# A graph attention layer on one core: weights loaded beside the projections, and the first sort, turn and chain put elsewhere

## The chip, the cores and the metric

The kernel runs on one core of a Trainium2 chip. The metric is the device time of one execution in microseconds (us), as the median of several runs; less is better. A core has TensorE (PE; its weight loads are listed as PEld), VectorE (DVE), ScalarE (ACT), GpSimd (POOL) and SyncE (SP). They run their own instruction queues in order and wait for each other by semaphores. SP, ACT and POOL also issue DMA transfers; "ACTq" is an instruction of ACT's queue that is not computation.

## The reference

One layer of a graph network on 4096 nodes of 512 features, with 8 heads of 64. The adjacency matrix is 4096 x 4096 of int32 with about 0.4% ones (made symmetric, with the diagonal), so a row has some 8 to 39 neighbours.

```
hs = layer_norm(x) * ln1_scale + ln1_bias ;  ht = layer_norm(h_target) * ln1_scale + ln1_bias
q = (ht @ Wq + bq) / 8 ;  k = hs @ Wk + bk ;  v = hs @ Wv + bv
probs = softmax over s of (q . k, where adj[t, s] != 0)          # per head
ht = layer_norm(ht + (probs @ v) @ Wo + bo) * ln2_scale + ln2_bias
out = _layernorm(x + ht + gelu(ht @ W1) @ W2)                    # W1: 512 x 2048, W2: 2048 x 512
```

All of it is in float32.

## The kernel before

The kernel doesn't multiply full matrices of 4096 x 4096: it makes neighbour lists out of the adjacency, sorts the target rows by their number of neighbours, and gathers the k|v rows of the neighbours slot by slot. P is 128; a row tile is 128 rows, so there are 32.

**Stage 1, projections** (`project`, L853). x is read two row tiles at a time. `measure` takes means and variances on DVE, `scale` normalizes on ACT, `turn` transposes on PE and copies out of PSUM with scale and bias on ACT (L896), `source` multiplies with Wk and Wv on PE (L906; an fp32 matmul is recorded as two), copies the result to an SBUF tile `tq` on ACT (L908) and writes 128 rows of k|v to the DRAM table `kvd` by a DMA of ACT's queue (L910). The gathers of attention need the whole table.

**Stage 1, lists** (`edges`, L703). A tile's adjacency comes in four quarters of 128 x 1024 by DMAs of SP's queue (L700) into slots of a ring of 17 buffers `kv` of 128 x 1024 floats; DEEP of them are used for that. ACT takes the sign and counts (L715), DVE multiplies with an index and takes maxima (L720, L722) and merges candidates (L729 to L746). The target rows are read beside it for their moments (`moments`, into ring slots by `hrow`). After the lists of the first 16 tiles (part A), `prepare` takes the moments of all targets and calls `sort(0)` (L794): one-hot rows of the degree (L814), counts by matmuls with ones and a running sum on DVE (L825, L826), ranks within a degree by matmuls with a lower triangle (L833, L834), and the rank (L837, L839). POOL then scatters the records of part A to DRAM, one DMA for each of 16 tiles (L842). `first_fronts` reads the first records, gathers target rows, normalizes them on ACT (L967), turns them and makes q (L980, L982). Meanwhile `fill` does lists of FILL = 5 tiles of part B.

**Stage 2, attention** (`attention`, L1104). The sorted tiles form 17 groups: one tile with 11 slots, then pairs with a nearly constant sum. A step has up to S = 3 slots. `issue` (L1001) gathers, by an indirect DMA of POOL's queue for each slot (L941), 128 rows of k|v into the ring, AHEAD = 4 steps before use. DVE multiplies with q (L1158) and reduces to logits `lg` (L1162), ACT takes exponentials (L1166, L1176) and weighs one slot of v (L1141), DVE the others (L1121), and PE adds up over transposes in PSUM (L1129). `finish` (L1021) is a generator: the chain at the end of a tile (sums, context, Wo, second norm, turned rows `h2T`), cut in pieces by `yield`, of which `advance` runs one each time, twice a step, so that no engine waits in its queue for the chain.

**Stage 2, feed forward** (`feed`, L1251). When a group's `h2T` is there, PE does `hidden` (L1266), ACT gelu (L1269), PE `output` (L1275), and `end` closes the rows with a norm and a scatter to the output. W1 and W2 are kept in four quarters, of 1 MB each from either matrix. `load_quarter` loads quarters 0 and 1 on SP's queue beside projections 8 and 10; `weights`, a stream of stage 2, loads 2 and 3 on ACT's queue. The memory of quarter 3's pool (`s2wb`, right side) and of quarter 2's (`s2wa`) is free only when the pools of stage 1 are closed: `wp` with R0 (the records of part A), `ip`, and `kvw` with Wk and Wv.

**Order.** `_weave` runs the streams of a stage by virtual time: a `yield` of a cost puts its stream later. That gives the order in which instructions are written; a planner of the framework then orders each engine's queue by that order, by what is ready, and by its own estimates of durations. In the last weave `other_lists` does the remaining tiles and `sort(1)`.

## Time and profile before

| | |
|---|---|
| median of 6 runs | 1877.92 us (1874.34 to 1881.0) |
| the profiled execution | 1879.3 us, span 1877.5 us |
| granted PE clock, mean | 0.967 |
| busy: PE, DVE, ACT, POOL | 1696.5 (90%), 1432.3 (76%), 1247.2 (66%), 890.5 (47%) us |
| moved by DMA | 463.28 MB, mean 247 GB/s |

Times in the profile are us from the span's start. A row of the timeline has start, duration, engine, line, operation, output and inputs with their shapes, how many were merged, and in brackets how long the engine was idle before and who released it. The releaser is inferred from semaphores: where several are waited for, the last one is named. A row in the table of stretches gives each engine's busy time and number of instructions, the clock that TensorE was granted (1.00 is full), the mean busy share of the 16 DMA engines, and GB/s. A busy PE isn't always PE at its peak, as matmuls are pipelined.

Landmarks: the projections' first matmul starts at 15.73, the lists of part A end at 197.5, rank is there at 245.3, the last k|v rows are issued at 300.5, the first gather at 308.7; attention starts on DVE at 319.5, the first feed at 375.0, the second at 448.4, and the last output row is scattered at 1863.

### The profile page before, as it was taken

What the parts mean: (1) busy time and instruction counts of PE and PEld (TensorE: products, weight loads), DVE (VectorE), ACT (ScalarE), POOL (GpSimd) and SP (SyncE); (2) the same over time, 40 slices, a digit from 0 to 9 for tenths busy, and PEclk for the clock granted to TensorE, in tenths of its full rate; (3) what the DMA queues carried; (4) which work ended last, traced back from release to release, by engine and by line L of the source; (5) the groups of instructions that cost most, each with busy time, mean ns of one, the idle gap of its engine ahead of it and who ended that gap; (6) DMA issues with size and microseconds to landing.
All of it is one profiled execution on the core that took longest, in us unless ns stands there. A gap on an engine that the chain in (4) does not pass through costs nothing. (4 is left out here: it accounts for less than half of the span.)

```text
span 1877.5 us, 22938 instructions
## 1 busy us (share of the span) xinstructions
PE 1696.5 (90%) x7030; PEld 1092.6 (58%) x7030; DVE 1432.3 (76%) x2591; ACT 1247.2 (66%) x3139; POOL 890.5 (47%) x804
## 2 busy tenths in 40 slices
PE   7989884598998989999989989899999999999996
PEld 3444331465666657666666656566666666656664
DVE  7989854989998838787878889888877878777400
ACT  6767634577886737777777777677767677777411
POOL 1000143746445474656566666655555555655101
PEclk9999987799999989999999999999999999999998
DMA  9999958878877657778778788777677867666000
GB/s 347 359 387 372 354 164 312 322 263 316 319 272 254 208 161 235 257 245 269 254 262 270 261 269 290 242 245 247 214 240 230 266 201 249 225 219 223 23 1 24
DMA packets 147757, 463.28 MB, mean 247 GB/s; under 512 B 24468, under 2 KB 29160, under 8 KB 147624
## 3 DMA queue, kind: packets, MB, share of 16 engines
q0 software_dynamic: 95696, 342.19, 53.8%
q1 hardware_dynamic: 44112, 96.44, 14.6%
q10 hardware_dynamic: 7816, 23.08, 3.2%
q8 instruction: 58, 0.95, 0.2%
q14 instruction: 75, 0.61, 0.1%
HBM read 430.76 MB, written 30.89 MB: 246 GB/s over the span
## 5 line engine op out<-in xcount | busy, mean ns | idle before, releaser
L941 POOL DMA_INDIRECT kv<-kvd,rec x603 | 690.2, 1145 | 487.3 <-PE cps L1129 205.4
L1266 PE MATMUL pf<-h2T,w 128*128 128x256 f32 (+1 forms) x2176 | 472.1, 369 | 2.2 <-issue 1.6
L1275 PE MATMUL po<-w,gt 128*128 128x512 f32 x1024 | 469.4, 599 | 0.3 <-issue 0.3
L1158 DVE TENSOR_TENSOR kv<-kv,tq 128x1536 f32<-128x1536 f32 (+2 forms) x211 | 352.4, 1676 | 112.5 <-DMA kv<-kvd,rec 82.5
L1266 PEld LDWEIGHTS pf<-h2T,w 128*128 128x128 f32 x2176 | 388.6, 191 | 66.3 <-issue 22.0
L1141 ACT ACTIVATE kv<-kv,pa 128x64 f32<-128x64 f32 x1520 | 391.5, 336 | 3.7
L1162 DVE TENSOR_REDUCE lg<-kv 128x24 f32<-128x1536 f32 (+2 forms) x211 | 350.7, 1669 | 1.8 <-ACT pa L1138 0.3
L1129 PE MATMUL cps<-ident,kv 128*128 128x128 f32 x2008 | 263.9, 278 | 59.5 <-DMA kv<-kvd,rec 20.5
L1129 PEld LDWEIGHTS cps<-ident,kv 128*128 128x128 f32 x2008 | 236.4, 143 | 135.7 <-issue 83.8
L1275 PEld LDWEIGHTS po<-w,gt 128*128 128x128 f32 x1024 | 188.1, 193 | 189.5 <-issue 188.8
L1121 DVE TENSOR_TENSOR kv<-kv,p 128x1024 f32<-128x1024 f32 (+1 forms) x211 | 249.6, 1190 | 46.3 <-ACT p L1166 33.7
L674 POOL TENSOR_TENSOR n_rs<-n_ve,mhalf 128x2 f32<-128x2 f32 (+2 forms) x51 | 51.6, 1011 | 331.9 <-DVE n_ve L667 132.4
L1269 ACT ACT_TABLE_LOAD x111 | 142.4, 1283 | 1.7
L980 PE MATMUL t<-wq,tq 128*128 128x512 f32 x256 | 121.1, 617 | 16.7 <-ACT tq L974 12.8
L906 PE MATMUL pq<-wk,h2T 128*128 128x512 f32 x256 | 124.0, 628 | 11.6 <-ACT h2T L896 6.2
L722 DVE MAX8 cand<-sg 128x8 uint16<-128x103 uint16 (+1 forms) x640 | 130.8, 252 | 0.7
L1269 ACT ACTIVATE gt<-pf 128x512 f32<-128x512 f32 x128 | 76.4, 597 | 72.4 <-PE pf L1266 58.5
L906 PE MATMUL pq<-wv,h2T 128*128 128x512 f32 x256 | 118.3, 604 | 6.8 <-ACT tq L908 6.8
L1056 PE MATMUL t<-wo,rb 128*128 128x512 f32 x256 | 118.3, 606 | 1.4 <-DVE rb L1046 1.4
L715 ACT ACTIVATE sg<-kv 128x1024 uint8<-128x1024 int32 x84 | 88.6, 1056 | 43.5 <-DVE cand L722 20.6
L906 PEld LDWEIGHTS pq<-wk,h2T 128*128 128x128 f32 x256 | 50.2, 203 | 77.3 <-issue 58.6
L1166 ACT ACTIVATE p<-lg 128x24 f32<-128x24 f32 (+2 forms) x179 | 33.7, 188 | 91.5 <-DVE lg L1162 73.3
(154 smaller groups left out, 1601.2 us busy)
## 6 DMA issues: line engine op xcount, KB each, us to landing
kv<-in_adj_dram SPq DMA_DIRECT2D x84, 512.0 KB
a<-in_adj_dram SPq DMA_DIRECT2D x44, 512.0 KB
kvd<-tq ACTq DMA_DIRECT2D x32, 512.0 KB
kv<-kvd,rec POOLq DMA_INDIRECT x603
kv<-in_L_gnn_h_target_dram SPq DMA_DIRECT2D x32, 256.0 KB
kv<-in_x_dram SPq DMA_DIRECT2D x15, 512.0 KB
rest_d<-gid SPq DMA_DIRECT2D x32, 160.0 KB
w<-in_L_gnn_W_dram SPq DMA_DIRECT2D x4, 1024.0 KB
```

Source lines behind the costliest of these rows:

```text
L722: nc.vector.max(cand[:, h * SQ + s, :], wd[:, w0:w1])
L906: nc.tensor.matmul(pkv, hT[:, kc, j * P:(j + 1) * P], w[:, kc, :], start=kc == 0, stop=kc == KC - 1)
L941: nc.gpsimd.indirect_dma_start(out=dst, out_offset=None, in_=table[:, :], in_offset=bass.IndirectOffsetOnAxis(ap=idx, axis=0))
L980: nc.tensor.matmul(pq, hT[:, kc, :], wq[:, kc, :], start=kc == 0, stop=kc == KC - 1)
L1121: nc.vector.tensor_tensor(v4, v4, p[:, j0:j0 + m, :].unsqueeze(3) .to_broadcast([P, m, H, HD]), ALU.mult)
L1129: nc.tensor.matmul(cps[:, c, :], kv[:, j, D + c * P:D + (c + 1) * P], ident, is_transpose=True, start=j0 + j == 0 and c == 0, stop=j0 + n ...
L1141: nc.scalar.mul(v, v, pa[:, hd:hd + 1])
L1158: nc.vector.tensor_tensor(kv[:, :n, :D], kv[:, :n, :D], tq[:, :D].unsqueeze(1).to_broadcast([P, n, D]), ALU.mult)
L1162: nc.vector.tensor_reduce(lg[:, :n, :], kv[:, :n, :D].rearrange("p j (h d) -> p j h d", h=H), AX.X, ALU.add)
L1266: nc.tensor.matmul(pf[:, k, :], w1[(f0 + k) // KC][:, kc, (f0 + k) % KC * P:((f0 + k) % KC + 1) * P], h2T[:, kc, :w], start=kc == 0, stop= ...
L1269: nc.scalar.activation(gt, pf, AF.Gelu_apprx_tanh)
L1275: nc.tensor.matmul(po[j], gt[:, k, j * P:(j + 1) * P], w2[(f0 + k) // KC][:, (f0 + k) % KC, :], start=False, stop=f0 + k == FC - 1, skip_g ...
```

## The change

- Quarters 0, 1 and 2 of W1 and W2 are loaded on SP's queue beside projections 6, 8 and 10, in the pool `wp2`. The stream `weights` is gone. Quarter 3 is loaded on ACT's queue in `attention` at step 1, after two one-column copies on ACT that read that step's `lg`.
- To make room, the pools `wp` and `ip` are gone. Their tiles are now parts of ring slots 7 (constants and moments) and 11 (the records R0 and the one-hot rows of the first sort), or of the pool `sp`.
- The adjacency has 7 ring slots (0 to 6) instead of 8, the target rows 3 (8 to 10) instead of 4.
- When the target rows are done, `source` uses ring slots 8 to 10 for k|v instead of the three buffers `tq`.
- The first rows are copied out of PSUM by DVE instead of ACT in `turn(0)`.
- `advance` runs three pieces of a chain until the first `h2T` is there.
- `fill` starts 9 units of virtual time later.

```diff
-            DEEP = 8
+            DEEP = 7
...
+            first_rec = ring[:, 11, :NA * RW].bitcast(I32).rearrange("p (n w) -> p n w", w=RW)
+            first_oh = ring[:, 11, 512:512 + NB * NA // 2].bitcast(BF16)
...
-            def load_quarter(pool, q, engine=nc.sync):
+            def load_quarter(pool, q, engine=nc.sync, gate=None):
                 w1.append(pool.tile([P, KC, D], F32, name=f"w1_{q}"))
                 w2.append(pool.tile([P, KC, D], F32, name=f"w2_{q}"))
+                if gate is not None:
+                    nc.scalar.copy(w1[q][:, 0, 0:1], gate)
+                    nc.scalar.copy(w2[q][:, 0, 0:1], gate)
                 engine.dma_start(w1[q], W1[:, q * D:(q + 1) * D].rearrange("(c p) n -> p c n", p=P))
...
             def hrow(i):
-                return ring[:, DEEP + i // 2 % 4, i % 2 * D:(i % 2 + 1) * D]
+                return ring[:, 8 + i // 2 % 3, i % 2 * D:(i % 2 + 1) * D]
...
-                            nc.scalar.activation(hT[:, kc, :], pt[:, k, :], AF.Identity,
-                                                 bias=b1c[:, kc:kc + 1], scale=s1c[:, kc:kc + 1])
+                            if n == 0:
+                                nc.vector.tensor_scalar(hT[:, kc, :], pt[:, k, :],
+                                                        s1c[:, kc:kc + 1], b1c[:, kc:kc + 1],
+                                                        op0=ALU.mult, op1=ALU.add)
+                            else:
+                                nc.scalar.activation(hT[:, kc, :], pt[:, k, :], AF.Identity,
+                                                     bias=b1c[:, kc:kc + 1],
+                                                     scale=s1c[:, kc:kc + 1])
...
-                    kvr = sp.tile([P, 2 * D], F32, name="tq", bufs=3)
+                    if asked or moms:
+                        kvr = sp.tile([P, 2 * D], F32, name="tq", bufs=3)
+                    else:
+                        kvr = ring[:, 8 + (n * G + j) % 3, :]
...
                     for t in list(tails):
-                        if next(t, StopIteration) is StopIteration:
-                            tails.remove(t)
+                        for _ in range(1 if h2Ts or begun else 3):
+                            if next(t, StopIteration) is StopIteration:
+                                tails.remove(t)
+                                break
+                    if h2Ts:
+                        begun.add(True)
...
+                            if k == 1:
+                                load_quarter(s2wa, NQ - 1, nc.scalar, lg[:, 0, 0:1])
...
-                    if n in (8, 10):
-                        load_quarter(wp2, n // 2 - 4)
+                    if n in (6, 8, 10):
+                        load_quarter(wp2, n // 2 - 3)
...
                 while not ready:
                     yield None
+                yield 9.0
                 for cost in _take(ed, FILL * steps):
...
-            def weights():
-                for q, pool in enumerate(pools):
-                    yield 10.0
-                    load_quarter(pool, q + 2, nc.scalar)
...
-            _weave((att, 0), (chain(feed(g) for g in range(len(GROUPS))), 0), (other_lists(), WAIT),
-                   (weights(), 0))
+            _weave((att, 0), (chain(feed(g) for g in range(len(GROUPS))), 0), (other_lists(), WAIT))
```

## The prediction

> **What bounds the kernel now.** The chain that ended last was read first. Its 11 pieces all lie behind 1860 us of a span of 1877.5 and say nothing about the start, where every edit of this change lies. So the busy time by stretches comes next (columns: us; busy us and count of PE, PEld, DVE, ACT, POOL; granted PE clock; DMA share; GB/s).
>
> ```profile
> 140.00:180.00 40.00, 40.00 (x112) 19.02 (x111) 38.59 (x169) 30.56 (x57) 2.06 (x3) 1.00 1.00 370
> 240.00:260.00 20.00, 20.00 (x60) 9.66 (x59) 18.77 (x74) 9.57 (x18) 11.18 (x11) 0.99 0.31 104
> 260.00:280.00 20.00, 14.28 (x28) 5.85 (x27) 3.76 (x16) 6.16 (x12) 9.81 (x12) 0.83 0.60 177
> 280.00:300.00 20.00, 12.96 (x31) 5.78 (x30) 8.32 (x35) 10.34 (x22) 0.39 (x1) 0.87 0.69 230
> 300.00:320.00 20.00, 9.47 (x16) 3.46 (x14) 7.60 (x26) 6.23 (x12) 8.54 (x10) 0.76 0.99 345
> 320.00:340.00 20.00, 5.64 (x24) 4.84 (x24) 19.23 (x25) 7.21 (x31) 16.43 (x12) 0.52 1.03 410
> 480.00:600.00 120.00, 117.00 (x528) 80.24 (x527) 115.42 (x255) 99.18 (x241) 64.59 (x56) 1.00 0.84 292
> ```
>
> Until about 200 us PE and DMA are both full; from 480 on PE is full again. Between lies a hole: from 260 to 340 PE is busy 42 of 80 us and its clock falls to 0.52. What fills the hole is in the timeline, engine by engine.
>
> ```profile
> 172.42 0.60 PE L892 MATMUL t<-ident,kv 128*128 128x128 f32 x4
> 187.03 0.60 PE L892 MATMUL t<-ident,kv 128*128 128x128 f32 x4
> 235.48 0.48 PE L825 MATMUL t<-oh,ones_bf 128*128 128x384 bf16 x1 [6.56 <-DVE a L826]
> 269.17 6.31 PE L906 MATMUL pq<-wv,h2T 128*128 128x512 f32 x8 [5.72 <-ACT tq L908]
> 285.13 1.12 PE L971 MATMUL t<-ident,tq 128*128 128x128 f32 x4 [2.78 <-ACT tq L967]
> 374.97 0.80 PE L1266 MATMUL pf<-h2T,w 128*128 128x128 f32 x2
> 448.40 1.97 PE L1266 MATMUL pf<-h2T,w 128*128 128x256 f32 x4 [0.66 <-ACT h2T L1086]
> ```
>
> The first two rows give the pace of the projections when nothing holds them: one pair of row tiles in 14.6 us, back to back. So PE sets their end. The next three are its losses; the last two are the first group's feed forward (375) and the second's (448), from where PE stays full.
>
> ```profile
> 268.05 0.39 ACTq L573 DMA_DIRECT2D w<-in_L_gnn_W_dram  x1
> 268.54 0.59 ACT L908 COPY tq<-pq 128x512 f32<-128x512 f32 x1 [14.20 <-DMA rec<-R,ranki]
> 300.51 0.33 ACTq L910 DMA_DIRECT2D kvd<-tq  x1
> ```
> ```profile
> 245.78 1.74 POOL L842 DMA_INDIRECT rec<-R,ranki  x1 [39.21 <-DVE ranki L839]
> 308.71 0.94 POOL L941 DMA_INDIRECT kv<-kvd,rec  x1 [28.32 <-issue]
> ```
> ```profile
> 319.49 1.76 DVE L1158 TENSOR_TENSOR kv<-kv,tq 128x1536 f32<-128x1536 f32 x1 [3.95 <-DMA kv<-kvd,rec]
> ```
>
> ACT stood 14.20 us in front of a load of weights. It must be quarter 3: the memory of quarter 2 is that of Wk and Wv, in use until 295. That of quarter 3 holds R0, which the scatter of the records still reads. Behind it in ACT's queue lay the copy that empties PE's accumulators. The last k|v rows go out at 300.51; only then can POOL gather (308.71), and attention begins on DVE at 319.49.
>
> **The change, part by part.** Times are of this execution: 1879.3 us, span 1877.5, so 1.8 lie around it; it is 1.4 over the median 1877.92. Ends of each term stand in brackets; minus is a gain.
>
> First turned rows on DVE. The first projection starts at 15.73, behind ACT's scaling of the next rows at 14.41. The eight transposes end at 9.89. Four DVE operations of 128x256 from PSUM follow; the nearest rows are 0.56 for DVE's 128x384 from PSUM (L834) and 0.56 for ACT's own operation, so about 2 us: start near 11.6. PE then runs back to back, so all of it passes on: -4 [-5; 0 if the weights wk, issued at 2.87, land late]. DVE's wait for PE holds the next rows' statistics, which have 10 us of slack before their turn at 25.74.
>
> A third quarter beside the projections: 2.1 MB more where the DMA share is 1.00. SP's queue is moved past by two issues of 0.4 to 1.2 us; behind them are adjacency and x loads. The same load at 187 is followed by PE gaps of 0.70, 1.05 and 0.36 at 203 to 212; the one at 153 by none. At 370 GB/s it is 5.7 us of DMA. I take +2 [0; +5.7], as the rows of the like load are nearest. The ring of seven adjacency buffers instead of eight goes into that bound. The Trainium skill (DMA: Bandwidth & Descriptors, "Issuing engines are not separate DMA queues") says that transfers of all queues run on the same 16 DMA engines and interleave, so that nothing is won by the queue and a full stretch would pay the whole 5.7; by it the sum below would be -17.
>
> The first sort ahead of the lists. Now it takes from 198 to 245.3, with 214.59 to 234.50 between its one-hot rows and its scan, filled by list operations; PE waits 6.56 for that scan. From the turn at 219.16 to the one at 244.37 PE takes 25.2 instead of 14.6. Of these 10.6, some 1.7 are the sort's four matmuls, and waits in PE's order will leave some 3: -6 [-9; 0]. Rank and scatter should come 20 us earlier, which shortens nothing by itself: the gathers wait for the last k|v rows. The lists pushed back cost DVE time later (below).
>
> No weight load on ACT behind the scatter. From the turn at 258.98 PE needs three tiles of 6.87 and 0.87 for turning, so 280.5; the last matmul ends at 295.4: 14.9 lost. The 14.20 us hold gives 5.72 of waiting and 2.7 of half-rate matmuls (6.31 against 3.60). The rest is the first front: 2.78 of waiting, 1.0 of transposes, slow clock. With records 20 us earlier most of that goes too: -11 [-14; -4].
>
> Last k|v rows. From the last matmul to the first gather are 13.3 us, with a wait for a tq buffer (3.15) and a weight load in the same queue just ahead (297.26). The buffers in ring slots take the first away: -3 [-6; 0].
>
> The last quarter, gated by the second step of attention: ACT gets two copies of one column and two issues (0.39 and 0.47 now). +1 [0; +4.4: ACT stood 4.36 at 274.59 behind a weight load]. Its 2.1 MB fall into the first gathers (share 1.03), but no other load lies before the first of them; four steps of gathers are ahead of DVE: +2 [-2; +5.7]. The Trainium skill (same page, "Queues, rings and completion order") has each engine alternate between queues by packets, so that gathers get half the rate while the load lasts; by it this term would be near +5.7. In this execution a weight load lies only ahead of the first gathers, so no row shows it beside four steps of them.
>
> Triple steps. The first chain takes from 343.27 to 374.45, in turns of one step; the durations in it add up to about 15. It can start the feed 10 to 13 us sooner. But the second feed waits for the second group, and from 319 to 448 DVE is busy 119.7 of 129: it sets that end. So the cover is DVE's work, and only its 9.3 idle us can come back: -3 [-9; 0].
>
> List work. From 262 to 319 DVE did 17.6 us in 57. With attention 20 us earlier, less of it is done beforehand: +1 [0; +10, one tile's lists being about 10].
>
> Sum: -4 + 2 - 6 - 11 - 3 + 1 + 2 - 3 + 1 = -21: attention near 297, the second feed near 427. From there PE is 97% busy (117.00 of 120) and its work is unchanged, so the end moves as much: 1858.3, and 1857 on the scale of the median. All good ends together give -45, all bad ones +22.
>
> **The rivals.**
> The gain is half eaten by DVE: two tiles of lists (20 us) fall behind attention's start and DVE, with 9.3 idle us in 129, pays 11 of them. For it: DVE's 115.42 of 120 at 480. Against: DVE has 49 idle us from 199 to 319. 1868.
>
> The order does not change: the sort's matmuls still queue behind projections, and list operations still fill the gap. Then the sort's 6 and half of the front's part (3) are missing: 1866.
>
> The first chain pays in full and the lists are ready: -9 instead of -3, and the good ends of the last rows and the hold (-6 more): 1845.
>
> Slower: ACT's hold is not removed but exchanged. The scaling of the first front (L967) stands in ACT's queue among projection copies. Before, it waited 5.16 us. With the sort moved ahead it may be queued right after rank, and then has the whole row of scatters (16 at 1.26), the wait for them (1.8), the read of the records (6.0) and the gather (7.2) before it: 35 us. PE can go on for two tiles' halves, some 7, and stands 28. With the front's own 4 that is 32 lost instead of 14.9, so +17 in place of -11: the sum is +7, about 1885. It decides from a hold of some 28 us. Against it: all four steps shift together.
>
> **How the numbers follow.** A measurement of this kernel tells 0.2% (3.8 us) from no change. Chances: my forecast 0.50; half eaten 0.14; order unchanged 0.09; all pays 0.10; exchange of the hold 0.11; costs and gains cancel within 0.2% 0.06. The first four are faster: 0.83; same 0.06; slower 0.11. The range goes from 1838, beyond the case in which all pays, to 1876, short of the last two.
>
> **What would show it.** Right: no ACT wait on the scatter; projections ending near 276, first gather near 286, attention near 297, second feed near 427 with PE full behind it. Wrong: a wait of over 10 us of ACT for the front's rows or of PE for copies; a second feed moved less than attention (DVE pays); PE gaps of over 5 us between 120 and 200 (the third quarter pays).

## The result and the profile after

| | before | after |
|---|---|---|
| median | 1878.65 us (74 runs) | 1885.32 us (33 runs) |
| ratio | | 1.0033 [1.0025, 1.0042] |
| profiled execution | 1879.3 us | 1878.07 us, span 1876.3 us |

The changed kernel is 0.33% slower, some 6 us, where 21 us less were forecast. Its profiled execution lies near the low end of its runs (1876.8 to 1889.99), so this pair of profiles doesn't show the 6 us. A second profile of either kernel (`again`, 1882.57 us; `before_again`, 1877.06) is read beside them. Line numbers are now those of the changed kernel (L923 was L906, L984 L967, L1180 L1158, L1291 L1266).

The stretches first, as in the prediction (us; busy us and count of PE, PEld, DVE, ACT, POOL; granted PE clock; DMA share; GB/s).

```profile
140.00:180.00 40.00, 40.00 (x113) 19.04 (x112) 36.05 (x149) 27.41 (x51) 2.07 (x3) 1.00 1.01 377
240.00:260.00 20.00, 20.00 (x61) 9.77 (x60) 18.54 (x76) 12.32 (x24) 11.56 (x12) 1.00 0.60 209
260.00:280.00 20.00, 14.44 (x28) 5.58 (x27) 9.83 (x41) 8.77 (x16) 10.23 (x12) 0.85 0.50 120
280.00:300.00 20.00, 13.88 (x38) 6.18 (x37) 12.89 (x52) 11.77 (x24) 0.00 (x0) 0.98 0.74 223
300.00:320.00 20.00, 3.07 (x8) 1.05 (x6) 12.11 (x40) 5.41 (x11) 11.40 (x12) 0.70 0.88 328
320.00:340.00 20.00, 5.65 (x24) 4.85 (x24) 16.88 (x26) 9.97 (x39) 13.07 (x10) 0.50 1.03 406
480.00:600.00 120.00, 114.13 (x519) 79.44 (x519) 108.54 (x231) 98.40 (x236) 62.55 (x56) 0.99 0.78 270
```

The hole from 260 to 340 is still there: PE is busy 37 of 80 us (42 before). The timeline of PE, then ACT, POOL and DVE of the same execution:

```profile
13.12 3.75 PE L923 MATMUL pq<-wk,h2T 128*128 128x512 f32 x4 [3.33 <-DMA wk<-in_L_gnn_Wk_dram]
23.94 0.33 PE L898 MATMUL t<-ident,kv 128*128 128x128 f32 x1 [1.29 <-ACT kv L885]
236.23 0.33 PE L831 MATMUL t<-kv,ones_bf 128*128 128x384 bf16 x1 [2.19 <-DVE a L832]
243.56 0.60 PE L898 MATMUL t<-ident,kv 128*128 128x128 f32 x4
275.60 6.26 PE L923 MATMUL pq<-wv,h2T 128*128 128x512 f32 x8 [5.20 <-ACT tq L984]
288.67 0.66 PE L988 MATMUL t<-ident,tq 128*128 128x128 f32 x4 [2.93 <-ACT tq L991]
365.70 0.71 PE L1291 MATMUL pf<-h2T,w 128*128 128x128 f32 x4
448.23 2.07 PE L1291 MATMUL pf<-h2T,w 128*128 128x256 f32 x4 [0.70 <-ACT h2T L1103]
```
```profile
274.26 0.81 ACT L984 ACTIVATE tq<-tq,rec 128x512 f32<-128x512 f32 x1 [5.45 <-DMA tq<-in_L_gnn_h_target_dram,rec]
```
```profile
245.09 1.18 POOL L848 DMA_INDIRECT rec<-kv,ranki  x1 [32.57 <-DVE ranki L845]
305.25 0.94 POOL L958 DMA_INDIRECT kv<-kvd,rec  x1 [28.47 <-DMA a<-in_adj_dram]
```
```profile
315.60 1.76 DVE L1180 TENSOR_TENSOR kv<-kv,tq 128x1536 f32<-128x1536 f32 x1 [3.82 <-issue]
```

The first projection is 2.6 us earlier; what it waits for last is the landing of wk. But the second turn, at 23.94, waits for ACT's scaling of its rows (before, it came at 25.74 without a wait). The scatter of the records is hardly earlier (245.09 against 245.78). The 14.20 us hold for a weight load is gone. ACT stands 5.45 us in front of the first front's scaling (L984). Before, it stood there 5.16 us, 10 us later, and PE's gap behind that was 2.78 us. Now a copy that empties PE's accumulators lies behind the wait, and PE's gap there is 5.20 us, where the load's hold had left 5.72. The projections end at 292.8 (295.4), attention starts at 315.6 (319.5). The first feed is 9 us earlier, the second is not (448.2 against 448.4).

Landmarks of all profiled executions, in us ("second group closed" is the start of the last DVE row that adds its residual, L1247; "last" that of the last group but one: the last group, a single tile, adds its own 28.5 us later in every kernel):

| | projections end | first gather | attention | first feed | second feed | second group closed | last |
|---|---|---|---|---|---|---|---|
| before, before_again | 295.4, 295.1 | 308.7, 306.3 | 319.5, 315.9 | 375, 372 | 448, 447 | 543, 542 | 1830, 1828 |
| after, again | 292.8, 295.6 | 305.3, 304.4 | 315.6, 315.9 | 366, 365 | 448, 449 | 546, 551 | 1829, 1834 |
| before_pool_load | 296.6 | 308.6 | 319.9 | 375 | 449 | 551 | 1837 |
| before_no_holds | 290.5 | 310.4 | 318.8 | 375 | 452 | 553 | 1841 |
| fronts_last | 284.5 | 300.6 | 312.7 | 361 | 447 | 553 | 1829 |
| no_last | 293.5 | 305.8 | 318.2 | 364 | 450 | 548 | 1835 |
| before_ring_of_seven | 298.8 | 310.2 | 319.7 | 375 | 452 | 546 | 1831 |
| before_triple | 292.9 | 305.4 | 315.9 | 362 | 451 | 546 | 1836 |
| ring_of_eight | 293.6 | 303.3 | 314.1 | 364 | 447 | 548 | 1836 |
| gate_step_9 | 290.6 | 302.8 | 313.9 | 361 | 453 | 554 | 1837 |
| third_at_step_9 | 300.6 | 309.3 | 321.2 | 371 | 460 | 571 | 1856 |
| single_steps | 292.0 | 302.3 | 313.2 | 374 | 451 | 548 | 1832 |
| q_early | 293.2 | 299.6 | 311.9 | 364 | 446 | 543 | 1835 |
| triple_two_chains | 293.2 | 303.7 | 314.9 | 365 | 444 | 541 | 1838 |
| all_early | 282.8 | 301.0 | 313.9 | 363 | 437 | 533 | 1834 |
| before_all_early | 288.5 | 309.0 | 327.6 | 377 | 453 | 550 | 1852 |
| late_fronts_q_early | 281.5 | 301.8 | 314.1 | 364 | 451 | 551 | 1836 |
| late_fronts_q_early_ring8 | 288.2 | 301.4 | 313.2 | 362 | 445 | 541 | 1829 |

Two things stand in this table. The projections' end moves by 19 us between kernels; the second feed lies within 445 to 453 us in all of them but three, whatever the projections do: it is later where two quarters are loaded inside attention (460), and earlier in two of the three kernels where two tail chains are tripled (437, 444). And from the second group's closing to the last column it takes 1276 to 1292 us in all kernels but three (all_early 1301, before_all_early 1302, triple_two_chains 1297). These 16 us are more than the 6 us looked for: a kernel that closes its second group early doesn't end early for it (triple_two_chains 541 and 1838, fronts_last 553 and 1829). Each row is one execution, and some lie far from the median of their kernel: fronts_last and single_steps were profiled in their fastest run, late_fronts_q_early_ring8 in its slowest, q_early near its slowest. So the table shows where work moved; it doesn't show where a few us of the median went.

The first 260 us need points of their own. A turn is PE's transposition of the rows of a pair (L892, in the changed kernel L898); there are 16.

| us | before, before_again | after, again | third_at_step_9 | before_ring_of_seven | ring_of_eight |
|---|---|---|---|---|---|
| first projection starts | 15.7, 15.8 | 13.1, 11.9 | 11.4 | 15.4 | 10.9 |
| third turn | 40.3, 39.7 | 39.2, 40.7 | 38.6 | 39.1 | 41.0 |
| 14th turn, ahead of the sort's wait | 219.2, 219.0 | 224.3, 220.3 | 222.0 | 223.1 | 216.9 |
| 15th turn, behind it | 244.4, 243.5 | 243.6, 242.3 | 245.6 | 247.6 | 241.3 |
| rank written (end of L839, now L845) | 245.5, 244.6 | 244.8, 243.5 | 245.5 | 248.7 | 242.3 |
| scaling of the first front (L967, now L984) | 284.3, 283.3 | 274.3, 272.9 | 277.7 | 288.2 | 271.8 |

### The profile page after: what moved, and what is told of

It is laid out like the page before. It is cut to its first block, busy times and chain, and to the rows that moved or that the text cites. A ratio compares the mean times of both kernels' runs of the same rounds, so it can differ in the third digit from the quotient of the medians.

```text
span 1876.3 us, 22937 instructions
## 1 busy us (share of the span) xinstructions
PE 1699.6 (91%) x7030; PEld 1096.6 (58%) x7030; DVE 1435.7 (77%) x2595; ACT 1238.7 (66%) x3131; POOL 882.7 (47%) x804
## 5 line engine op out<-in xcount | busy, mean ns | idle before, releaser
L1291 PE MATMUL pf<-h2T,w 128*128 128x256 f32 (+1 forms) x2176 | 471.4, 369 | 3.9 <-issue 3.2
L1180 DVE TENSOR_TENSOR kv<-kv,tq 128x1536 f32<-128x1536 f32 (+2 forms) x211 | 352.0, 1677 | 108.9 <-DMA kv<-kvd,rec 89.6
L1291 PEld LDWEIGHTS pf<-h2T,w 128*128 128x128 f32 x2176 | 388.9, 191 | 68.1 <-issue 23.9
L1151 PE MATMUL cps<-ident,kv 128*128 128x128 f32 x2008 | 267.1, 281 | 60.5 <-DVE kv L1143 39.7
L681 POOL TENSOR_TENSOR n_rs<-n_ve,mhalf 128x2 f32<-128x2 f32 (+1 forms) x50 | 42.6, 853 | 327.7 <-DVE n_ve L674 153.0
L1294 ACT ACT_TABLE_LOAD x108 | 138.6, 1283 | 1.6
L997 PE MATMUL t<-wq,tq 128*128 128x512 f32 x256 | 118.2, 604 | 14.9 <-ACT tq L991 9.1
L923 PE MATMUL pq<-wk,h2T 128*128 128x512 f32 x256 | 123.2, 625 | 9.4 <-DMA wk<-in_L_gnn_Wk_dram 3.3
L923 PE MATMUL pq<-wv,h2T 128*128 128x512 f32 x256 | 119.6, 611 | 10.9 <-ACT tq L925 5.7
L923 PEld LDWEIGHTS pq<-wv,h2T 128*128 128x128 f32 x256 | 49.9, 197 | 75.1 <-issue 60.1
```

The lines of the kernel that those rows point to most:

```text
L923: nc.tensor.matmul(pkv, hT[:, kc, j * P:(j + 1) * P], w[:, kc, :], start=kc == 0, stop=kc == KC - 1)
L1151: nc.tensor.matmul(cps[:, c, :], kv[:, j, D + c * P:D + (c + 1) * P], ident, is_transpose=True, start=j0 + j == 0 and c == 0, stop=j0 + n ...
L1180: nc.vector.tensor_tensor(kv[:, :n, :D], kv[:, :n, :D], tq[:, :D].unsqueeze(1).to_broadcast([P, n, D]), ALU.mult)
L1291: nc.tensor.matmul(pf[:, k, :], w1[(f0 + k) // KC][:, kc, (f0 + k) % KC * P:((f0 + k) % KC + 1) * P], h2T[:, kc, :w], start=kc == 0, stop= ...
L1294: nc.scalar.activation(gt, pf, AF.Gelu_apprx_tanh)
```

## The experiments

Ratios are to the kernel before on the same chip, with a 95% interval. Two sets of runs of the changed kernel gave 1.0033 and 1.0021, so a difference of 0.15% between two kernels tells little.

**The change again.** A second profile of the changed kernel and of the one before.

> The changed kernel once more, unedited, for a second profile and as the measure of the other three. Known: 1885.3 us in the median against 1878.7 before, a ratio of 1.0033. If the loss lies in the start, a profile near the median shows the second feed forward near 455 instead of 448.2. If it lies in the steady part, the second feed begins near 448 again and the steady part to the last output row takes some 6 us more.

> The kernel before, unedited, for a second profile. It shows how far the landmarks move by themselves: first gather 308.7, attention 319.5, second feed 448.4 and last projection 295.4 in the first profile. I expect each within 2 us.

again: 1.0021 [1.0006, 1.0036].

```profile
272.86 0.81 ACT L984 ACTIVATE tq<-tq,rec 128x512 f32<-128x512 f32 x1 [12.80 <-DMA tq<-in_L_gnn_h_target_dram,rec]
```

Here ACT's hold before L984 is 12.80 us and the projections end at 295.6, where they ended before; the second group closes 7 to 8 us later than in the two profiles of the kernel before and the last column 3 to 6 later. The same kernel's projections thus end 2.8 us apart in two profiles, and the kernel before's first gather 2.4: a smaller difference between two rows of the table tells little.

**The hold on ACT, taken alone.** The term of -11 was the largest of the sum.

```diff
 # before_pool_load: the kernel before
-                    load_quarter(pool, q + 2, nc.scalar)
+                    load_quarter(pool, q + 2, nc.gpsimd if q else nc.scalar)
```


> The kernel before with one thing else: the last quarter's load beside the projections (L573, L574 with q = 3) is issued on POOL's queue, behind the scatter and the reads of rec that it waits for, instead of on ACT's queue. This is the term of -11 us of my prediction taken alone. Theory A (exchange): the wait of 14.20 us on ACT goes, but ACT then stands in front of L967 for the first gather (5.2 us before, up to 13 us now), the projections end 1 to 6 us earlier than 295.4, and the time is 1874 to 1879 us. Rival B (the term was right as it stood and something else in the change ate it): projections end at 284 to 286, time 1867 to 1870. Rival C (nothing in this stretch sets the time): projections end earlier, time within 2 us of 1878.7.

1.0037 [1.0019, 1.0055]: slower. ACT's and PE's timeline of this kernel (before's lines):

```profile
276.00 1.06 ACT L715 ACTIVATE sg<-a 128x1024 uint8<-128x1024 int32 x1 [7.44 <-DMA a<-in_adj_dram]
283.44 0.81 ACT L967 ACTIVATE tq<-tq,rec 128x512 f32<-128x512 f32 x1 [3.70 <-DMA tq<-in_L_gnn_h_target_dram,rec]
```
```profile
277.67 2.07 PE L906 MATMUL pq<-wv,h2T 128*128 128x512 f32 x2 [7.53 <-ACT tq L908]
```

The 14.20 us hold is gone and two others stand in its place: the sign rows of the part B lists wait 7.44 us for adjacency, the front 3.70 for its gather. PE's gap is 7.53 us, where it was 5.72. The projections end at 296.6, 1.2 to 1.5 later than in the two profiles of the kernel before. Taken alone, without the earlier rank, the term of -11 is worth nothing.

**First fronts behind the last projection.** In the changed kernel, and in the kernel before with the load on POOL.

```diff
 # fronts_last: after; before_no_holds: before_pool_load with the same edit
-                yield from first_fronts()
+                for i in range(EARLY):
+                    prefetch(i)
...
             _weave((projections(), 0), (prepare(), 0), (fill(), 0))
+            for _ in first_fronts():
+                pass
...
+                with tc.issue_after(last[-1].ins):   # the last k|v write
                     nc.scalar.activation(t, t, AF.Identity, bias=m[:, 1:2], scale=m[:, 0:1])
```


> The changed kernel with one thing else: the first fronts (gather of h_target L958, scale L984, turns L988, scale L991) are put behind the last projection, so ACT no longer stands in front of L984 for its gather while PE waits for ACT's copies. Theory A (the hold that was on ACT in front of the weight load has been exchanged for a hold on the first fronts' gather, and that is why the projections' end did not move): the waits of 5.4 us (first profile of the changed kernel) and 12.8 us (second profile) and PE's gaps of 5 and 4 us behind them go, the projections end at 283 to 287 us instead of 292.8 to 295.6, the first gather comes at 295 to 299, attention starts at 305 to 309, and the time falls by 5 to 9 us against the changed kernel's 1883 to 1885 us: 1875 to 1879 us. Rival B (PE's projections are late from earlier, by the ring and the lists, and the tail only shifts): projections end earlier by less than 3 us, time as the changed kernel's, 1882 to 1886. Rival C (the start of attention does not set the time, DVE and the 2.1 MB beside the first gathers do): projections end 6 to 9 us earlier, but the second feed's pf stays at 447 to 450 us and the time stays at 1881 to 1886.

> The kernel before with both: the load of q = 3 on POOL's queue as in the other run, and the first fronts behind the last projection. No hold of ACT's over 2 us is left from 245 to 295 us except those of the ring and the lists. Theory A: the 14.2 us, 5.2 us and 1.6 us go from ACT's row; projections end at 278 to 283 us instead of 295.4, the first gather comes at 289 to 294, and the time falls by 8 to 13 us: 1866 to 1871 us, faster than both kernels. Rival C (what attention does between its start and the second feed sets the time, by DVE, not its start): projections end at 278 to 283, but the stretch from attention's start to the second feed grows from 129 us to 138 us or more, and the time stays at 1876 to 1880 us.

fronts_last: 1.0021 [1.0006, 1.0037], as the changed kernel's own 1.0021; before_no_holds: 1.0069 [1.0046, 1.0092], slower. PE and DVE of fronts_last:

```profile
296.42 1.11 PE L990 MATMUL t<-ident,tq 128*128 128x128 f32 x4 [11.93 <-ACT tq L986]
```
```profile
312.65 1.76 DVE L1182 TENSOR_TENSOR kv<-kv,tq 128x1536 f32<-128x1536 f32 x1 [4.25 <-issue]
```

The projections end 8.3 us earlier than in the changed kernel, the first gather comes 4.7 earlier, attention 2.9, the second feed 1.3, and the time stays. Some of the way is lost on ACT, which waits on sign rows of the lists (3.21, 2.29 and 1.76 us, for adjacency and for DVE) between the last copies, so that the last k|v write is issued at 294.56. The rest is lost behind attention's start, as rival C said. In before_no_holds the projections end 5 us earlier, but ACT waits for adjacency between the last copies (2.30, 1.77, 3.52 us), the last k|v write goes out at 300.32 as before, and attention starts at 318.8 (319.5 and 315.9 before). Why it is 0.7% slower is not settled. Theory A's sum fell in both.

**The last quarter beside the first gathers.**

```diff
 # no_last: two columns are loaded, quarter 2's weights are used (it leaves out the right weights of a quarter)
+                if gate is not None:
+                    engine.dma_start(w1[q][:, 0, 0:2], W1[0:P, 0:2])
+                    engine.dma_start(w2[q][:, 0, 0:2], W2[0:P, 0:2])
+                    w1[q], w2[q] = w1[q - 1], w2[q - 1]
+                    return
 # gate_step_9
-                            if k == 1:
+                            if k == 9:
```


> The changed kernel without the last quarter's load beside the first gathers: only two columns of it are read and the third quarter's weights are used in its place, so this kernel leaves out 2.1 MB of transfer and the right weights of a quarter of the feed's channels. It prices that transfer where the change has put it. Theory A (the 2.1 MB take the DMA engines from the kv gathers and DVE from its work): DVE's busy time in 320 to 360 us goes from 35 back to 38 or 39 us, the second feed's pf comes at 443 to 445 us instead of 448, and the time falls by 4 to 6 us to 1878 to 1881 us. Rival B (the transfer is hidden): 1882 to 1886 us, as the changed kernel.

> The changed kernel, with the last quarter of the weights gated by step 9 of attention instead of step 1, so its 2.1 MB no longer lie beside the first gathers. Theory C (the load halves the gathers' rate): DVE waits less for gathered rows between 315 and 360, the second feed comes 4 to 6 us sooner, near 443, and the time falls by as much. Theory D (DVE has four steps of gathers ahead, the load is hidden): no difference above 2 us.

no_last: 1.0058 [1.0036, 1.0079]; gate_step_9: 1.0033 [1.0016, 1.005]. The stretch from 320 to 360 us of before, after and no_last:

```profile
320.00:360.00 40.00, 16.50 (x82) 13.19 (x83) 39.05 (x46) 20.14 (x80) 31.83 (x25) 0.67 0.98 376
```
```profile
320.00:360.00 40.00, 18.04 (x74) 13.89 (x75) 34.85 (x43) 18.79 (x72) 22.70 (x19) 0.59 1.01 400
```
```profile
320.00:360.00 40.00, 18.54 (x91) 14.18 (x92) 37.91 (x46) 22.56 (x85) 26.36 (x21) 0.68 0.92 358
```

The load does take DVE's time there (third busy number: 39.05, 34.85, 37.91 us), as theory A said. But without it the kernel is no faster, so those 3 us wait elsewhere when they are saved. Why no_last is slower than the changed kernel is not settled.

**Three quarters beside the projections, or two.**

```diff
 # third_at_step_9: quarter 2 at step 1, quarter 3 at step 9
-                            if k == 1:
-                                load_quarter(s2wa, NQ - 1, nc.scalar, lg[:, 0, 0:1])
+                            if k in (1, 9):
+                                load_quarter(s2wa if k > 1 else s2wb, 2 if k == 1 else 3, nc.scalar, lg[:, 0, 0:1])
...
-                    if n in (6, 8, 10):
-                        load_quarter(wp2, n // 2 - 3)
+                    if n in (8, 10):
+                        load_quarter(wp2, n // 2 - 4)
```


> The changed kernel, with only quarters 0 and 1 beside the projections (8 and 10), quarter 2 at step 1 and quarter 3 at step 9 of attention. It takes 2.1 MB out of the full stretch of stage 1. Theory E (the third quarter pays in full where DMA is full): the lists of part A end 5.7 us earlier, the PE gap of 5.68 near 100 and others go, projections end near 287 instead of 292.8, and the time falls by 4 to 6. Theory F (PE sets the pace and swallows it): no difference above 2 us.

1.0115 [1.0095, 1.0135]: 0.8 to 0.9% slower than the changed kernel. The projections end 8 us later, the second feed comes 12 later and its group closes at 571. But the table of the first 260 us shows no gain from the load that is gone, and the late projections' end has another cause:

```profile
277.69 0.81 ACT L984 ACTIVATE tq<-tq,rec 128x512 f32<-128x512 f32 x1 [19.05 <-DMA tq<-in_L_gnn_h_target_dram,rec]
```

ACT stands 19.05 us in front of the first front (5.45 and 12.80 in the changed kernel), so the run prices two things at once: the loads inside attention and a longer hold. That the third quarter is better off beside the projections is therefore not shown by it. Which of the two loads inside attention does harm was not tried.

**Seven or eight slots for the adjacency.** The first run also takes the target rows from four slots to three, as the change does; the second leaves them at three.

```diff
 # before_ring_of_seven
-            DEEP = 8
+            DEEP = 7
...
-                return ring[:, DEEP + i // 2 % 4, i % 2 * D:(i % 2 + 1) * D]
+                return ring[:, 8 + i // 2 % 3, i % 2 * D:(i % 2 + 1) * D]
 # ring_of_eight: after, its constants in tiles of the pool sp instead of slot 7
-            DEEP = 7
+            DEEP = 8
```


> The kernel before with seven adjacency slots and three for target rows, nothing else. Theory G: a PE gap of 5 to 7 near 100 instead of 1.7, and slower by 3 to 6 us. Theory H: the gap comes, the time stays within 2 us.

> The changed kernel with eight adjacency slots again (0 to 7): the constants and moments go into two buffers of the pool sp that stage 1 does not use, everything else stays. Theory G (the seventh slot missing is what lets ACT wait for adjacency while Wo and Wq pass, and PE behind it): ACT's wait near 97 falls from 6.1-7.6 to about 4.3, PE's gap near 100 from 5.7 to about 1.7, projections end near 288, and the time falls by 3 to 6, to 1879 to 1882. Theory H (the gap is made up later, since the gathers wait for something else or DVE sets the pace until the second feed): the gap goes, the time stays within 2 us of the changed kernel.

before_ring_of_seven: 1.0029 [1.0014, 1.0045]; ring_of_eight: 1.0017 [0.9997, 1.0037]. ACT's row at the same place, in the kernel before and with seven slots:

```profile
97.02 1.06 ACT L715 ACTIVATE sg<-kv 128x1024 uint8<-128x1024 int32 x1 [4.31 <-DMA kv<-in_adj_dram]
```
```profile
96.31 1.06 ACT L715 ACTIVATE sg<-kv 128x1024 uint8<-128x1024 int32 x1 [8.53 <-DMA kv<-in_adj_dram]
```

Wo and Wq are issued on SP's queue at 79 to 80 us, ahead of adjacency. With the shorter ring ACT's wait for adjacency behind them is 4.2 us longer; it is 7.61 and 6.06 us in the two profiles of the changed kernel and 5.65 in ring_of_eight. PE's gap behind it is 3.75 us (1.72 with eight), 5.68 in the changed kernel, 0.19 in ring_of_eight.

The price shows best from the third turn to the 14th. With eight slots PE takes 177.3 to 180.7 us in the six profiles of the kernel before and its variants, and 175.9 and 175.6 in the two that give the changed kernel its slot back and keep three loads and three target slots. With seven it takes 184.0 in before_ring_of_seven and 179.6 to 185.9 in the eleven profiles of the changed kernel and its variants, 183.4 among them with two loads only (third_at_step_9). So the slot costs some 5 to 7 us there, and neither the third load nor the target slot shows a cost. But most of it ends at the sort, for which PE waits ahead of the 15th turn: this turn comes at 240.5 to 245.6 in all profiles but that of before_ring_of_seven (247.6). Taken alone, the shorter ring costs the kernel before nearly what the whole change costs. Given back, the slot makes the changed kernel no faster by more than the noise.

**Triple steps.**

```diff
 # single_steps: after; before_triple: before with the change's three steps; triple_two_chains: after
-                        for _ in range(1 if h2Ts or begun else 3):
+                        for _ in range(1):                              # single_steps
+                        for _ in range(1 if len(begun) > 1 else 3):     # triple_two_chains
...
+                    begun.update(h2Ts)                                  # triple_two_chains
```


> The changed kernel, with the first chain in single steps again. Theory A (my forecast's term of -3: the triple steps help a little): slower than the changed kernel by 0 to 9 us, first feed near 375 or later. Theory B (the triple steps put feed forward and the last quarter's use where attention of the second group needs PE and ACT): faster than the changed kernel by 3 to 6 us, second feed earlier than 448.

> The kernel before with triple steps of the first chain, nothing else. My forecast's term is -3 [-9; 0]: first feed near 363 instead of 375, second feed 448 or up to 9 us sooner. Against the run with single steps (slower than the changed kernel by 4 to 5): if the triple steps are worth that by themselves, the time is 1874. Rival: the second feed is set by DVE, so it stays at 448 and so does the time.

> The changed kernel with triple steps for the first two tail chains, not for the first alone. Theory A (from the third tile's end at 409 us to the second feed at 448 us the chain is paced by its single steps, 25 us of them up to the matmuls with wo): the stretch from the third tile's reciprocal to its matmuls with wo falls from 25 us to 10 to 15, the second feed starts at 432 to 440 us, the time falls by 5 to 10 us to 1874 to 1880. Rival B (DVE's work of attention and lists sets the second feed; chain steps only change places with it): second feed at 440 to 448, its end where it was (546 to 551), time 1881 to 1887.

single_steps 1.0062 [1.0042, 1.0083], before_triple 1.0011 [0.9996, 1.0026], triple_two_chains 1.0056 [1.003, 1.0081]. The first feed is 8 to 13 us earlier with triple steps; the second is some 2 earlier in the changed kernel and 3 to 4 later in the one before. The changed kernel has 1.0021 in the same set of runs as single_steps, and 1.0033 over all: there triple steps gain 0.3 to 0.4%, 5 to 8 us, while on the kernel before they gain nothing. DVE and PE of the changed kernel show what is late behind the earlier feed; the last row is DVE's of single_steps:

```profile
356.04 2.35 DVE L1180 TENSOR_TENSOR kv<-kv,tq 128x1536 f32<-128x1536 f32 x2
380.97 0.67 DVE L999 SCALAR_TENSOR_TENSOR tq<-t,bqr 128x512 f32<-128x512 f32 x1
381.74 1.74 DVE L1180 TENSOR_TENSOR kv<-kv,tq 128x1536 f32<-128x1536 f32 x1
```
```profile
373.74 1.73 PE L1291 MATMUL pf<-h2T,w 128*128 128x128 f32 x14 [0.93 <-issue]
375.31 1.02 PE L997 MATMUL t<-wq,tq 128*128 128x512 f32 x2
```
```profile
361.03 0.69 DVE L999 SCALAR_TENSOR_TENSOR tq<-t,bqr 128x512 f32<-128x512 f32 x1 [1.80 <-PE t L997]
```

L1180 is attention's multiplication. None runs from 358.4 to 381.7: it needs the third tile's q (L999), whose matmuls (L997) stand in PE's queue behind 10 us of the first feed, and DVE does mostly lists meanwhile. With the feed later (before, and single_steps, which has L999 at 361.03) the third tile's q is made ahead of it. What this hole costs is not shown: single_steps doesn't have it and is slower. With triple steps for both chains the second feed is 4 us earlier and the time is longer: theory A fell in its size and its sign.

**The third tile's q ahead of the first feed.**

```diff
 # q_early: after
-            EARLY = 2
+            EARLY = 3
```


> The changed kernel with three first fronts in place of two (EARLY 3 for 2), so that the third tile's q (matmuls L997) lies on PE ahead of the first feed's pf. Theory A (with triple steps the first feed stands in PE's order in front of the third tile's q, DVE has no multiplication L1180 from 356 to 382 us, and this eats the 10 us of the earlier feed): L1180 goes on after 356 us with a gap under 15 us, the third tile's end (reciprocal L1050) comes at 395 to 400 us instead of 409, the second feed at 436 to 442 instead of 448, the time falls by 5 to 10 us to 1874 to 1880. Rival B (DVE's sum of work sets the stretch; what is taken from the gap is paid as list work later): the gap shrinks, the second feed stays at 446 to 450 us, time 1881 to 1886. Rival C (a third front costs ACT one more wait ahead of the last projections): projections end 2 to 6 us later and the time is 1884 to 1889.

0.9995 [0.9981, 1.001]: the change's loss is gone. DVE of q_early:

```profile
358.64 1.73 DVE L1180 TENSOR_TENSOR kv<-kv,tq 128x1536 f32<-128x1536 f32 x1
377.16 1.23 DVE L1180 TENSOR_TENSOR kv<-kv,tq 128x1024 f32<-128x1024 f32 x1 [2.70 <-DMA kv<-kvd,rec]
408.63 0.69 DVE L999 SCALAR_TENSOR_TENSOR tq<-t,bqr 128x512 f32<-128x512 f32 x1
```

The hole at 358 is filled, the third tile ends at 390.4 (409.2 in the changed kernel), but the next hole, without a multiplication until the fourth tile's q is there, goes from 378.4 to 409.6: 31 us, where the changed kernel has 23 and 14. The second feed is 2 us earlier, not 10. The time falls as theory A said, the way is rival B's. The edit also brings the first gather 5 to 6 us forward and attention 4. Which of this makes the time fall is not shown; the profiled run, 1883.98, is near the slowest of its kernel.

**Put together.**

```diff
 # all_early: fronts_last + q_early + triple_two_chains; before_all_early: the same on before
 # late_fronts_q_early: fronts_last + q_early
 # late_fronts_q_early_ring8: fronts_last + q_early + ring_of_eight
```


> The changed kernel with all three: first fronts behind the last projection, three of them, and triple steps for two chains. Theory A: the gains add; attention starts at 311 to 314 us, the second feed at 425 to 435 us, its end at 525 to 538 instead of 546, time 1862 to 1874, better than both kernels. Rival B: the second feed comes earlier by over 8 us but its end stays at 543 to 553 us, as DVE and PE are full there (93 and 94 of 100 us in 450 to 550), and the time stays at 1878 to 1886.

> The kernel before with the same three (first fronts behind the last projection, three of them, triple steps for two chains), and nothing of the change but the triple steps. Its loads on ACT and its 14.2 us hold stay. Theory A: the second feed starts at 430 to 440 us instead of 448, the time is 1868 to 1875. Rival B: as in the other runs, the second feed's end at 543 to 553 us, time 1877 to 1884.

> The changed kernel with first fronts behind the last projection and three of them (fronts_last and q_early together). Theory A (the gains add: q_early took 3 to 6 us off the changed kernel, fronts_last 0 to 3): 1873 to 1878 us, faster than both kernels by 0.1 to 0.3%. Rival B (the stretch from attention's start to the third feed is full on DVE; what comes earlier waits later): attention starts at 311 to 314 us, the third feed ends at 637 to 646 as in all kernels, time 1878 to 1883.

> The same with eight slots in the adjacency's ring (the small constants in other tiles). Theory A: another 0 to 3 us less than late_fronts_q_early. Rival B: no difference beyond 2 us, 1878 to 1883.

| kernel | median us | ratio |
|---|---|---|
| all_early | 1879.7 | 0.9995 [0.9975, 1.0014] |
| before_all_early | 1906.82 | 1.013 [1.0104, 1.0155] |
| late_fronts_q_early | 1884.92 | 1.0012 [0.9999, 1.0024] |
| late_fronts_q_early_ring8 | 1874.38 (before here 1881.68) | 0.9952 [0.9935, 0.9969] |

all_early starts the second feed 11 us earlier than the changed kernel and closes its group 13 earlier, and 1301 us follow where 1283 did: the gain is given back. late_fronts_q_early_ring8 is faster than both kernels, by 0.5% than the one before and, by the two ratios, by 0.7 to 0.8% than the changed one (0.9952 against 1.0021 and 1.0033). So the change's parts can pay with three further edits. It is one set of six runs. Which of the three does it is not settled: the eighth slot was worth 0.04 to 0.16% on the changed kernel and is worth 0.6% here, and in this profile the projections even end later (288.2) than without it (281.5). Seen is only that the fourth tile's q is made at 407.37 instead of 413.55, and that the second group closes at 541 instead of 551.

## Why the prediction was wrong

Attention was to start 22 us earlier. It starts at 315.6 and 315.9, against 319.5 and 315.9: 0 to 4 us earlier. The second feed moved even less, and in the second profile ACT waited over 10 us for the front's rows; both were named as signs of being wrong. So nearly all of the forecast was lost before attention's start, and most of it by one step.

**The sort, and rank 20 us earlier (-6).** This step failed first, and the hold's term rested on it. "Rank and scatter should come 20 us earlier": the cast of rank starts at 244.63 instead of 245.32. The one-hot rows came at 221.40 instead of 214.59, and list operations still lay between them and the scan (235.24). In all 20 profiles rank is written between 241.8 and 248.7. The rival "the order does not change" was right in this. PE's time between the two turns around the sort did shrink, from 25.2 and 24.5 us to 19.3 and 22.1, by what was forecast or half of it; but mainly because PE came to the sort 1 to 5 us later. The turn behind it is 1 us earlier.

**The hold (-11).** The argument took PE's 14.9 us as the load's and the front's, and let both go with an earlier sort. The front's scaling follows rank by scatter, records and gather: 29.2 to 30.3 us in eight of the nine profiles of the changed kernel and its variants that have the front among the projections, 32.2 in the ninth. So ACT passes L984 at 271.6 to 274.4 in the eight and at 277.7 in the ninth, and what it doesn't wait ahead of it, it waits there: 5.45 and 12.80 us in the two profiles of the changed kernel, 19.05 in third_at_step_9. By the prediction's own count (from the turn at 258.17 PE needs 21.5 us) the loss is 13.1 us in the changed kernel and 17.1 in its second profile: the term is -2 to +2. before_pool_load, which takes the load away alone, shows the same: each wait removed uncovers the next (front, adjacency, front). The exchange was named as the rival of the other sign, with a hold of 35 us; it came smaller. Its time, 1885, is the one measured; that is luck, as its sum was not.

**The first turned rows (-4)** gave -2.6 and -3.8 at the first projection, near the forecast, down to the named bound, the landing of wk. "All of it passes on" failed: by the third turn it is gone (39.2 and 40.7 against 40.3 and 39.7). DVE, busy with the first rows, brings the next rows' statistics later; their scaling starts at 23.07 instead of 14.41, and the second turn waits for it. The 10 us of slack were not enough.

**The last k|v rows (-3)** gave -1 to -2: from the last matmul to the first gather are 12.5 and 8.8 us against 13.3 and 11.2.

**The third quarter (+2)** was mis-sized because the ring of seven was counted into it. The gap it causes is at 100 us, 5.68 us long, at other weights. From the third turn to the 14th the shorter ring costs 5 to 7 us; the load itself shows no cost. The sort's wait hides most of it in the changed kernel.

**The last quarter (+1 and +2).** DVE's busy time beside it fell by 3.1 us (37.91 without the load, 34.85 with it), inside the range and short of the 5.7 that the prediction estimated from 370 GB/s and from what the Trainium skill (DMA: Bandwidth & Descriptors, "Queues, rings and completion order") says of engines alternating between queues. Left out, the load gave the time nothing.

**Triple steps (-3).** On the changed kernel undoing them costs 5 to 8 us, which is within the range forecast; taken alone on the kernel before they cost 2 us (-1 to 5). The forecast's reason, that only DVE's idle time can come back, doesn't explain this, and the other side was missed: an earlier feed stands in PE's queue ahead of the next tile's q, and DVE has 23 us without a multiplication of attention.

**The sum passes on.** Had attention started earlier, this step would have failed next. "The second feed near 427, and the end moves as much" supposed that attention takes the same 129 us. In the changed kernel it takes 132.6 and 133.2, in the one before 128.9 and 131.2. fronts_last, with projections 8.3 us earlier than the changed kernel, has 134 us from attention's start to the second feed; all_early closes its second group 13 us earlier and needs 18 us more from there. What sets the pace from 315 to 550 us was not isolated.

So it is known why the gain didn't come. Where the loss of 6 us comes from stays open: the four profiles of the two kernels show only 2 us of it on average. The parts don't add: the shorter ring alone costs the kernel before 5 us, triple steps help the changed kernel and not the one before, and q_early takes 5 to 7 us off the changed kernel without touching the slots.

## What to carry to other kernels

A wait in an in-order queue is worth only its distance to the next wait in that queue: list, behind the wait you remove, every row that has a releaser of its own, and when that releaser was done. Before a gain at the front of a pipeline is passed to the end, move that front by itself and look whether the end follows. When a step is made earlier, ask on each queue that it enters what it now stands in front of. And where one term of a sum is the condition of another, as rank was of the hold, look for what the condition itself waits for.

## What the runs showed that was not expected

A shorter ring of buffers cost its price not beside the loads that were argued about, but where two other weights passed (ACT's wait 8.53 us instead of 4.31), and a later wait that was there anyway hid most of it. ACT's hold in front of the first front was 5.45 us in one profile and 19.05 in another, while the front itself came only 3.4 us later. Removing 2.1 MB of transfer from the stretch where DVE waits for gathers gave nothing back. And three small edits that gave 0 to 0.1, 0.3 to 0.4 and 0 to 0.2% alone gave 0.7 to 0.8% together, while two of them together gave 0.1 to 0.2%.
